# Softmax denominators inverted once per head and query, in a transformer block on one Trainium2 core

## The chip, the cores and the metric

The kernel runs on one core of one Trainium2 chip. The metric is the device time of one execution in microseconds (us). Besides the timed runs there is one execution taken by the hardware profiler; all rows below are of that one. The engines are named as in the profile: PE (TensorE, matrix products; PEld are its weight loads), DVE (VectorE), ACT (ScalarE), POOL (GpSimd) and SP (the queue that issues most transfers).

## The reference, cut to what matters

One block of a transformer with adaptive layer norm, on x of 4 x 2048 x 256 in float32:

```python
h = layernorm(x) * (1 + ca) + sa
q, k, v = heads(h @ w_qkv)                       # 8 heads of 32
scores = q @ k.T / sqrt(32) + head_scale * q_proj * k_proj, causal
x = x + ga * (softmax(scores) @ v) @ w_out
h = layernorm(x) * (1 + cb) + sb
p = softmax(h @ router_w.T); gate = its 4 largest of 16, the rest 0
x = x + gb * (shared_experts(h) + sum over e of gate[e] * expert_e(h))   # gelu inside
```

The softmax divides, for each head and query, a sum over keys of exp(score - max) * v by the sum of exp(score - max), the denominator. This division is what the change rewrites.

## The kernel before, in words

The 8192 tokens are cut into 16 blocks of 512 queries; block i is query block qb = i % 4 of its batch row, so it looks at (qb + 1) * 4 tiles of 128 keys. Heads come in two groups g of four (NQ = 2), each head in 32 partitions.

Everything is emitted in an order written out by the program: each engine executes its instructions strictly in that order (`Pinned`, L41). The order comes from a planner with costs in us: `T_US, P_US, M_US, M_VE, S_US = 0.6, 1.8, 1.05, 2.7, 3.2`. Block i is emitted as a part i of two stretches, called fill i and sum i below.

- **Fill i** (`fill_in`, L517): "pieces" of PE work (projections of a later block, the output product of block i-1, the shared expert of block i-2, routed expert tiles) between "tops", the searches for row maxima of block i+1. One search is four score products on PE, a mask where needed, and two `TENSOR_REDUCE` of 128x1024 on DVE. The planner counts 1.05 us of PE and 2.7 or 3.4 us of DVE for it, and puts the first search when its clock passes `begin`. `begin` is 5.0, or, where a lead of projections comes first, the length of that lead plus 1. `whole = begin + sum(ve of all searches)`; routed expert tiles are taken into the fill by `take_tiles(max(whole - own, backlog - 90.0))`, where `own` is the planned time of the other pieces. Searches that find no cover are left to the sum.
- **Sum i** (`sum_steps`, L665): ks = 8 * (qb + 1) steps. A step makes scores again (tile `st`), subtracts the maxima by a small product, takes exp on ACT (tiles `p`), and adds p @ v into one PSUM tile (`av`) and p @ ones into another (`dv`). As `ones` is 128 x 32, every denominator stands 32 times: in the 32 partitions of its head, the query along the columns.

At the last key tile DVE copies the denominators to SBUF (`rd<-dv`, L746) and ACT copies the numerators (`oT<-av`). The two accumulators alternate in two PSUM tiles (`accp`), so the next head group's products, or the next fill's, wait for these copies. Then come four `divide` steps per head group (L750): a `RECIPROCAL` of 128x128 in place and a product of 128x128. Those of the first head group are put into the second half of the sum, those of the second (`ends`) between the first pieces of the next fill. `rd` has one buffer.

`put` (L1501) places DVE work beside the steps of a sum: every step has 2.2 us of `room` (1.4 beside a search), and a piece takes its cost from it; a `divide` counts 1.2. Where 2.2 us are left in two neighbouring steps, the kernel "joins": DVE adds two p tiles (two `TENSOR_TENSOR p<-p,p` of 128x1024), and one set of `dv` products serves both key tiles.

**Routing.** The 14 first blocks form groups of 2, 3, 3, 3 and 3. Once a group's last block has chosen its experts, `place_steps` gives every row its place, and POOL scatters the rows into a DRAM buffer (`xg<-rows,at`, one indirect DMA for 128 rows, each paced behind ACT's latest instruction). The calls stand in the list `scatters`, and `tick()` issues one of them at a time: once or twice a step of a sum, every 3.2 planned us in a fill. When the list is empty, which is looked at after a fill and after a sum, `tiles_of(group)` makes the group's expert tiles ready: from then on a fill may take them. A set of four tiles needs rows (`xr<-xg`, SP, which waits for all scatters of the group), weights of four experts (`wt<-experts`, SP, 4 x 256 KB), turns (`px`), up (`pu`), gelu, down (`py`) and a store (`yg<-y`). Rows and weights are fetched two sets ahead. The last fill, 15, takes whatever is left. Behind sum 15 stands the dense tail for the last two blocks, with the last group's tiles.

Of the kernel before, what the change touches and what calls it, by code (L numbers as in the profile page):

```python
# [12 lines left out]
F32 = mybir.dt.float32  # L13
# [6 lines left out]
P = 128  # L20
# [14 lines left out]
def run(placed):  # L35

    for _, step in sorted(placed, key=lambda p: p[0]):
        step()
# [54 lines left out]
def adaln_block_kernel(  # L93
# [405 lines left out]
    def tick(add=True):  # L499
        for due in sums_due:  # L500
            due[0] -= 1
        if add and sums_due and sums_due[0][0] <= 0:
            sums_due[0][1].pop(0)()
            if not sums_due[0][1]:
                sums_due.pop(0)
        if scatters:
            scatters.pop(0)()
            return
        if not gathers and ready and len(sums_due) < 2:
            gathers.extend(ready[0][0])  # L510
        if gathers:
            gathers.pop(0)()
            if not gathers:
                sums_due.append([3, ready.pop(0)[1]])
# [150 lines left out]
    def sum_steps(i, g, oT):  # L665


        qb = i % NB
        nkb = (qb + 1) * TT
        qT, mT = qTs[i], mTs[i, g]  # L670
        sums = []
        pts, held = {}, {}
        joining = set()

        def keys(kb):
            return (i - qb + kb // TT) % SLOTS, kb % TT

        def left(kb):
            return max(0, kb - qb * TT) * P

        def probabilities(kb):
            lo = left(kb)
            slot, n = keys(kb)
            halves = [pair(f"st{i}_{g}_{kb}_{a}") for a in range(2)]
            heads = [both[:, u, :] for both in halves for u in range(2)]
            for h in range(4):
                r = G * h
                nc.tensor.matmul(
                    heads[h][:, lo:],
                    lhsT=kT[r : r + G, slot, g, n * P : (n + 1) * P],  # L690
                    rhs=qT[r : r + G, g, lo:],
                    start=True,
                    stop=False,
                    tile_position=(r, 0),
                )
            for h in range(4):
                r = G * h
                nc.tensor.matmul(
                    heads[h][:, lo:],
                    lhsT=unit3[r : r + 3, :],  # L700
                    rhs=mT[r : r + 3, lo:],
                    start=False,
                    stop=(kb < qb * TT),
                    tile_position=(r, 0),
                )
            if kb >= qb * TT:
                for h in range(4):
                    nc.tensor.matmul(
                        heads[h][:, lo : lo + P],
                        lhsT=ident_b,  # L710
                        rhs=kmask,
                        start=False,
                        stop=True,
                    )
            pts[kb] = []
            for a, both in enumerate(halves):
                name = f"p{i}_{g}_{kb}_{a}"
                if kb in joining:
                    pt = probs.tile([P, 2, QB], F32, bufs=2, tag="joins", name=name)
                else:  # L720
                    pt = probs.tile([P, 2, QB], F32, tag="pt", name=name)
                nc.scalar.activation(pt[:, :, lo:], both[:, :, lo:], AF.Exp)
                pts[kb].append(pt)

        def weigh(kb, s):
            if len(sums) == s:
                sums.append(accp.tile([P, QB], F32, tag="acc", name=f"{'ad'[s]}v{i}_{g}"))
            lo = left(kb)
            slot, n = keys(kb)
            if s and kb + 1 in joining:  # L730
                return
            of = pts[kb - 1] if s and kb in joining else pts[kb]
            for h in range(4):
                r = G * h
                c0 = g * P + r
                nc.tensor.matmul(
                    sums[s][r : r + G, lo:],
                    lhsT=ones if s else vA[:, slot, n, c0 : c0 + G],
                    rhs=of[h // 2][:, h % 2, lo:],
                    start=(of is pts[0]),  # L740
                    stop=(kb == nkb - 1),
                    tile_position=(0, r),
                )
            if kb == nkb - 1 and s:
                held["rd"] = once.tile([P, QB], F32, tag="rd", name=f"rd{i}_{g}")
                nc.vector.tensor_copy(held["rd"], sums[1])  # L746
            elif kb == nkb - 1:
                nc.scalar.copy(oT[:, g, :], sums[0])

        def divide(t):  # L750
            own = slice(t * P, (t + 1) * P)
            rd = held["rd"]
            nc.vector.reciprocal(rd[:, own], rd[:, own])
            nc.vector.tensor_tensor(oT[:, g, own], oT[:, g, own], rd[:, own], ALU.mult)

        def join(kb):
            for one, other in zip(pts[kb - 1], pts[kb]):
                nc.vector.tensor_tensor(one, one, other, ALU.add)

        steps = [  # L760
            [
                lambda kb=kb: probabilities(kb),
                lambda kb=kb: weigh(kb, 0),
                lambda kb=kb: weigh(kb, 1),
            ]
            for kb in range(nkb)
        ]
        return steps, [lambda t=t: divide(t) for t in range(TT)], joining, join

    def out_steps(i, oT):  # L770

# [647 lines left out]
    for i in range(NBLK):  # L1419
# [4 lines left out]
        if i:  # L1424
            soon, later = projected_in(i)
            outs = out_steps(i - 1, oT)
            turns, ups, downs = [], [], []
            if i > 1:
                turns = turn_steps(i - 2)
                ups, downs = dense_steps(i - 2)  # L1430
            begin = 5.0
            lead, mid = [], []
            if soon:
                new = project_steps(soon[0])
                lead = new[:2] + turns[:2] + new[2:6]
                begin = sum(us for us, _ in lead) + 1.0
                mid = ups + turns[2:] + new[6:]
            elif later:
                new = project_steps(later[0])
                mid = new[:2] + turns[:2] + ups + new[2:3] + turns[2:] + new[3:]  # L1440
            else:
                mid = turns[:2] + ups + turns[2:]
            if soon and later:
                mid += project_steps(later[0])
            finals = [s for two in zip(downs, outs) for s in two] if downs else outs
            at = max(6, len(mid) - len(finals))
            tail = merged(mid[at:], finals) if mid[at:] else finals
            mid = mid[:at] + tail

            for n, s in enumerate(ends):  # L1450
                (lead or mid).insert(2 * n + 1, (0.001, s))
            tops = [] if last else maxima(i + 1)
            state["pairs"] = not last
            own = sum(us for us, _ in lead + mid)
            whole = begin + sum(ve for ve, _, _ in tops)
            backlog = sum(us for us, _ in tiles_to_come)
            now = take_tiles(1e9 if last else max(whole - own, backlog - 90.0))
            filler = own + sum(us for us, _ in now)
            m, busy = 0, begin
            while m < len(tops) and (  # L1460
                busy + tops[m][0] <= filler + 2.0 or len(tops) - m > int(0.9 * ks)
            ):
                busy += tops[m][0]
                m += 1
            rest = tops[m:]
            left = fill_in(lead + (merged(mid, now) if now and mid else mid), tops[:m], begin)
# [34 lines left out]
        def put(steps, lo, hi):  # L1501
            at, shift = int(lo), (hi - lo) / max(1, len(steps))
            for n, (us, wait, step) in enumerate(steps):
                at = min(max(at + wait, int(lo + n * shift)), ks - 1)
                while room[at] < us and at < ks - 1:
                    at += 1
                room[at] -= us
                part.append((at + 0.6, step))
            return at
# [2 lines left out]
            us = [0.6] * TT + [0.2] + [0.4] * TT + [0.0] * TT  # L1512
            return [(u, 1 if n == TT + 1 else 0, s) for n, (u, s) in enumerate(zip(us, steps))]

        put([(1.2, 0, s) for s in divided], ks // NQ + 1, ks // NQ + 1)
        if qb == 0:
            for j in fresh[:1]:
                put(norm(first_norm_steps(j)), 1, 1)
# [42 lines left out]
        if 0 < i < 4:  # L1561
            now = tables[:3] if i == 1 else tables[:8]
            tables = tables[len(now) :]
            part += [(when(length * (n + 0.7) / len(now)), s) for n, s in enumerate(now)]
        run(part)
        state["summing"] = False
        if filled is not None and not scatters:
            tiles_of(filled)
# [86 lines left out]
```

## Time and profile before

| what | us |
|---|---|
| timed runs, median of 3 | 2529.13 (2527.44 to 2539.77) |
| the profiled execution's own time | 2556.92 |
| its span, first to last instruction | 2555.2 |
| PE busy in it | 2384.5 (93%) |
| DVE busy in it | 1503.9 (59%) |
| mean granted PE clock | 0.955 |

The stretches by their first score and last score product of a block in the trace (us from the span's start): fill 9 1184.7 to 1298.3, sum 9 to 1344.8, fill 10 to 1398.1, sum 10 to 1506.7, fill 11 to 1555.7, sum 11 to 1657.2; fill 13 1757.4 to 1862.1, sum 13 to 1913.1, fill 14 to 1957.9, sum 14 to 2072.8, fill 15 to 2183.5, sum 15 to 2279.9, then the tail to 2555.2.

Nearly all instructions are recorded at one line, L52, because the helper `Pinned` issues them; they are told apart by their tiles. A group of the profile names line, engine, operation, out<-in, shapes and count, then the busy time and the mean ns of one, then the engine's idle time before them and what ended it. A row of the windows view gives a stretch, its length, the busy time and instruction count of PE, PEld, DVE, ACT and POOL, the granted PE clock, and the share and rate of the DMA engines. A matmul in float32 is recorded as two passes, and four of 32 rows or 32 columns run side by side.

### The profile page before, as it was taken

Reading aid. Unit: us, or ns where it says so; the run is one execution under the profiler, and the core shown is the slowest. Engines: PE = TensorE matmul, PEld = TensorE weight load, DVE = VectorE, ACT = ScalarE, POOL = GpSimd, SP = SyncE. Lnnn points to the kernel's source line nnn. Section 1 sums busy time; section 2 is a strip of 40 time slices with the busy share of each in tenths; the row PEclk is TensorE's granted clock in tenths of the full one; section 3 lists DMA queues with packets and bytes.
Section 4 is the critical chain, followed back from the end, with each engine's and each line's share of the span. In section 5 each row is a group of like instructions: output and inputs, shape, how many; then the busy total and the mean of one; then the engine's idle time right before and its main releaser. Section 6 shows DMA issues by size and latency. Waiting matters only on the chain. (4 is left out here: it accounts for less than half of the span.)

```text
span 2555.2 us, 42456 instructions
## 1 busy us (share of the span) xinstructions
PE 2384.5 (93%) x16713; PEld 1181.2 (46%) x16713; DVE 1503.9 (59%) x2895; ACT 980.1 (38%) x1391; POOL 714.9 (28%) x740
## 2 busy tenths in 40 slices
PE   7999999999999999999999999998998998998987
PEld 4443433345544333365645344364633257435754
DVE  5576665546667775547575657658557840552235
ACT  2324244543333344534353345533342344552320
POOL 3201010511124035201013333502353320454334
PEclk9989999999999899999999999998997999998999
DMA  3200403233532112233622145233623259337943
GB/s 118 87 1 9 149 9 124 104 133 111 179 100 65 34 50 95 71 116 121 211 96 75 51 142 160 86 125 113 224 88 103 63 181 305 127 118 265 332 147 115
DMA packets 219704, 306.90 MB, mean 120 GB/s; under 512 B 18544, under 2 KB 158832, under 8 KB 219504
## 3 DMA queue, kind: packets, MB, share of 16 engines
q1 hardware_dynamic: 192720, 228.89, 27.1%
q0 software_dynamic: 25536, 73.43, 9.0%
q8 instruction: 132, 2.16, 0.4%
q10 hardware_dynamic: 1248, 1.86, 0.2%
q14 instruction: 68, 0.56, 0.1%
HBM read 193.49 MB, written 114.82 MB: 121 GB/s over the span
## 5 line engine op out<-in xcount | busy, mean ns | idle before, releaser
L52 DVE TENSOR_REDUCE parts<-ps 128x2 f32<-128x1024 f32 (+3 forms) x640 | 662.4, 1063 | 314.6 <-PE ps L52 305.4
L52 ACT ACTIVATE p<-st 128x1024 f32<-128x1024 f32 (+3 forms) x640 | 538.9, 894 | 624.4 <-PE st L52 530.1
L52 PE MATMUL st<-qT,kv 32*128 32x512 f32 (+3 forms) x2560 | 423.6, 588 | 18.3 <-ACT p L52 11.7
L52 PE MATMUL ps<-kv,qT 32*128 32x512 f32 (+3 forms) x2560 | 398.8, 610 | 25.9 <-DVE parts L52 16.2
L52 POOL DMA_INDIRECT got<-yg,at x224 | 222.6, 994 | 358.3 <-ACT p L52 100.1
L52 PE MATMUL av<-p,kv 128*32 128x512 f32 (+3 forms) x2560 | 309.0, 549 | 4.4 <-DVE rd L52 2.0
L72 POOL DMA_INDIRECT xg<-rows,at x219 | 219.0, 1000 | 290.4 <-ACT p L52 121.3
L52 PEld LDWEIGHTS st<-qT,kv 32*128 32x128 f32 x2560 | 152.1, 186 | 282.6 <-issue 167.6
L52 PE MATMUL dv<-p,ones 128*32 128x512 f32 (+3 forms) x2312 | 267.7, 535 | 1.6 <-DVE p L52 1.6
L52 PEld LDWEIGHTS ps<-kv,qT 32*128 32x128 f32 x2560 | 133.9, 192 | 233.0 <-issue 99.1
L52 DVE TENSOR_TENSOR ps<-ps,cmask 128x256 f32<-128x256 f32 x256 | 109.3, 427 | 224.3 <-PE ps L52 187.7
L52 POOL TENSOR_TENSOR x<-x,tmps 128x512 f32<-128x512 f32 x28 | 35.4, 1263 | 520.2 <-DVE tmps L52 520.1
L52 PE MATMUL st<-mT,unit 3*128 3x512 bf16 (+3 forms) x1280 | 175.0, 348 | 0.0
L52 PE MATMUL pu<-xt,wt 128*128 128x128 f32 x1216 | 157.3, 280 | 16.3 <-DMA wt<-experts 14.5
L52 PE MATMUL py<-wt,tact 128*128 128x256 f32 x608 | 164.0, 403 | 8.8 <-DVE rd L52 1.9
L52 PEld LDWEIGHTS pu<-xt,wt 128*128 128x128 f32 x1216 | 148.8, 192 | 38.4 <-issue 13.9
L52 ACT COPY y<-py 128x512 f32<-128x512 f32 x152 | 89.0, 586 | 146.9 <-PE py L52 145.8
L52 PEld LDWEIGHTS py<-wt,tact 128*128 128x128 f32 x608 | 111.0, 196 | 51.2 <-issue 8.5
L52 PEld LDWEIGHTS dv<-p,ones 128*32 128x32 f32 x2312 | 63.5, 110 | 148.3 <-issue 137.1
L52 DVE RECIPROCAL rd<-rd 128x128 f32<-128x128 f32 x128 | 121.0, 945 | 0.9
L52 PEld LDWEIGHTS av<-p,kv 128*32 128x32 f32 x2560 | 53.8, 108 | 140.8 <-issue 117.0
L52 POOL TENSOR_TENSOR x<-x,tmp 128x512 f32<-128x512 f32 x32 | 40.5, 1267 | 278.1 <-DVE tmp L52 238.8
(289 smaller groups left out, 2588.9 us busy)
## 6 DMA issues: line engine op xcount, KB each, us to landing
wt<-experts SPq DMA_DIRECT2D x304, 256.0 KB
xr<-xg SPq DMA_DIRECT2D x76, 512.0 KB
yg<-y SPq DMA_DIRECT2D x76, 512.0 KB
xg<-zeros SPq DMA_DIRECT2D x16, 1024.0 KB
xin<-in_x SPq DMA_DIRECT2D x16, 512.0 KB
x<-in_x SPq DMA_DIRECT2D x16, 512.0 KB
h2d<-xnb POOLq DMA_DIRECT2D x14, 512.0 KB
pre<-x POOLq DMA_DIRECT2D x14, 512.0 KB
```

Source lines behind the costliest of these rows:

```text
L52: made = call(*args, **kwargs)
L72: made = call()
```

## The change

- The copy of the denominators becomes a DVE transpose: each square of 32 partitions by 32 columns is turned, so that a query stands in a partition and the 32 equal copies along the columns.
- `invert` takes the reciprocal of the first column of each of the 16 squares (128x16) into a small tile `each`; `back` turns squares made of that column repeated 32 times, and so puts the reciprocals where they are needed.
- `divide` remains a product, now two of 128x256. The four steps go where the four `divide` steps went; `put` counts 0.2, 0.7, 0.5, 0.5 instead of 1.2 each.
- `begin` of a fill without a lead is 2.5 instead of 5.0.
- After a sum, when one or two scatters are left, they are issued at once, so that `tiles_of` follows before the next fill instead of after it.

```diff
@@ -742,16 +742,28 @@
             if kb == nkb - 1 and s:
                 held["rd"] = once.tile([P, QB], F32, tag="rd", name=f"rd{i}_{g}")
-                nc.vector.tensor_copy(held["rd"], sums[1])
+                nc.vector.transpose(held["rd"], sums[1])
             elif kb == nkb - 1:
                 nc.scalar.copy(oT[:, g, :], sums[0])
 
-        def divide(t):
-            own = slice(t * P, (t + 1) * P)
-            rd = held["rd"]
-            nc.vector.reciprocal(rd[:, own], rd[:, own])
-            nc.vector.tensor_tensor(oT[:, g, own], oT[:, g, own], rd[:, own], ALU.mult)
+        def invert():
+            each = small.tile([P, QB // G], F32, bufs=1, tag="each", name=f"each{i}_{g}")
+            squares = held["rd"].rearrange("p (b j) -> p b j", j=G)
+            nc.vector.reciprocal(each, squares[:, :, 0])
+            held["each"] = each
+
+        def back():
+            squares = held["rd"].rearrange("p (b j) -> p b j", j=G)
+            wide = held["each"].unsqueeze(2).broadcast_to([P, QB // G, G])
+            nc.vector.transpose(squares, wide)
+
+        def divide(half):
+            own = slice(half * QB // 2, (half + 1) * QB // 2)
+            nc.vector.tensor_tensor(oT[:, g, own], oT[:, g, own], held["rd"][:, own], ALU.mult)
...
-        return steps, [lambda t=t: divide(t) for t in range(TT)], joining, join
+        return steps, [invert, back, lambda: divide(0), lambda: divide(1)], joining, join
@@ -1428,7 +1440,7 @@
-            begin = 5.0
+            begin = 2.5
@@ -1512,7 +1524,7 @@
-        put([(1.2, 0, s) for s in divided], ks // NQ + 1, ks // NQ + 1)
+        put([(us, 0, s) for us, s in zip((0.2, 0.7, 0.5, 0.5), divided)], ks // NQ + 1, ks // NQ + 1)
@@ -1563,6 +1575,8 @@
         run(part)
+        while filled is not None and 0 < len(scatters) <= 2:
+            tick()
         state["summing"] = False
         if filled is not None and not scatters:
             tiles_of(filled)
```

## The prediction

> **What bounds the kernel now.** First the page's busy times.
>
> ```profile
> PE 2384.5 (93%) x16713; PEld 1181.2 (46%) x16713; DVE 1503.9 (59%) x2895; ACT 980.1 (38%) x1391; POOL 714.9 (28%) x740
> ```
>
> PE is the bound and DVE is not, so DVE time saved is not time saved. Next the groups by form, for prices.
>
> ```profile
> L52 PE MATMUL dv<-p,ones 128*32 128x512 f32 x1544 | 206.6, 610 | 1.6 <-DVE p L52 1.6
> L52 DVE RECIPROCAL rd<-rd 128x128 f32<-128x128 f32 x128 | 121.0, 945 | 0.9
> L52 DVE TENSOR_TENSOR oT<-oT,rd 128x128 f32<-128x128 f32 x128 | 42.2, 330 | 6.8 <-DVE rd L52 0.5 <-ACT oT L52 0.2
> L52 DVE TENSOR_TENSOR sum<-sum,gbs 128x256 f32<-128x256 f32 x56 | 24.4, 435 | 0.8
> L52 DVE COPY rd<-dv 128x512 f32<-128x512 f32 x32 | 22.0, 687 | 89.0 <-PE dv L52 62.9 <-PE ptb L52 17.1 <-PE pta L52 8.9
> L52 DVE RECIPROCAL rsm<-rsm 128x4 f32<-128x4 f32 x16 | 2.9, 178 | 0.6
> ```
>
> Then the windows view, by stretch: fill 9, sum 11, fill 14, sum 14, fill 15, sum 15 (length; busy PE, PEld, DVE, ACT, POOL; clock).
>
> ```profile
> 1184.70:1298.30 113.60, 106.05 (x678) 69.71 (x670) 70.76 (x98) 38.97 (x68) 13.39 (x15) 0.97 0.62 203
> ...
> 1555.70:1657.20 101.50, 96.90 (x831) 30.50 (x830) 77.94 (x172) 59.43 (x68) 54.62 (x52) 0.97 0.35 106
> ...
> 1913.10:1957.90 44.80, 39.33 (x200) 21.09 (x192) 31.83 (x38) 5.70 (x10) 18.11 (x18) 0.79 0.43 144
> 1957.90:2072.80 114.90, 110.04 (x855) 33.69 (x854) 88.02 (x167) 43.45 (x51) 40.05 (x43) 0.96 0.20 61
> 2072.80:2183.50 110.70, 94.00 (x628) 81.30 (x620) 16.51 (x34) 49.03 (x89) 9.87 (x9) 0.98 0.85 283
> 2183.50:2279.90 96.40, 93.09 (x845) 30.36 (x845) 49.08 (x106) 58.32 (x67) 52.96 (x52) 1.00 0.29 91
> ```
>
> The average hides this: fill 14 has too little PE work (clock 0.79), sum 14 is then loaded with searches (DVE 88 of 115), and fill 15 has tiles and hardly any DVE work (16.5 of 111) while DMA is at 0.85. The waits view gives the reason for fill 15's idle PE:
>
> ```profile
> PE pu L52 <- DMA wt<-experts: 14.5, 17, 2.0
> ```
>
> Of these, 13.6 us lie in fill 15. Last the timeline after a group's last scatter, in the tail and where fill 14 begins:
>
> ```profile
> 2316.58 0.96 POOL L72 DMA_INDIRECT xg<-rows,at  x1 [0.30 <-issue]
> ...
> 2319.22 0.92 SPq L52 DMA_DIRECT2D xr<-xg  x2
> ...
> 2323.55 1.94 PE L52 MATMUL px<-ident,xr 128*128 128x128 f32 x8 [8.11 <-DMA xr<-xg]
> ```
> ```profile
> 1918.75 1.82 PE L52 MATMUL ptb<-ident,xnb 128*128 128x128 f32 x8 [2.39 <-ACT oT L52]
> ...
> 1921.47 0.96 POOL L72 DMA_INDIRECT xg<-rows,at  x1 [0.85 <-ACT h2T L52]
> ...
> 1923.88 0.92 SPq L52 DMA_DIRECT2D xr<-xg  x2
> ```
>
> From scatter to rows takes 2.6 + 4.3 us.
>
> **The division.** Per head group it cost 0.687 + 4 x (0.945 + 0.330) = 5.79 us of DVE. The reciprocal of 16 columns, from its two rows: (945 - 178) / 124 = 6.2 ns a column, 178 + 12 x 6.2 = 0.25 us. Two products at 0.435. No row shows a DVE transpose: below, the COPY of the same shape and source, 0.69; above, the reciprocal's rate, 0.178 + 508 x 0.0062 = 3.3 us. I take 0.69, since both only move data. New: 0.69 + 0.25 + 0.69 + 0.87 = 2.50, a saving of 3.29, 105 us of DVE over 32 head groups. (The Trainium skill, VectorE: DVE Perf Modes, "The three transpose paths", gives 311 ns for 128x128 in bf16; with 384 more columns at the COPY's 1.34 ns that is an estimate of 0.83 us, and 9 us more of DVE; no run here shows it.) PE hides nearly all of it. What shows are PE waits ended by `rd`, 8.4 us over the trace, four of them near 1.9 us (fills 5, 9, sum 5, fill 15): the copy stands on DVE behind older divides and the PSUM tile comes free late. 6.5 of them lie outside part 14/15; I take 5.
>
> **Joins.** `put` charges 1.9 instead of 4.8. Going through its rooms as written I get 39 joins for 31 (the 62 rows p<-p,p are 31 joins): 6 more in sum 14, 1 in sum 15, one net elsewhere. A join saves one `dv` set: 206.6 / 1544 x 4 = 0.53 us of PE.
>
> **begin.** Fills 1, 2 and 6 have more search than PE work, so the planner's clock, within 7% of the trace there (45.5, 52.0, 52.0 planned; 42.5, 49.0, 51.9 in the trace), falls by 1.8, 2.6 and 2.6. In fills 9 to 13 a few tiles and three searches change places (planned +1.3 for the fills; three searches fewer in sums, at (105.7 - 75) / 21 = 1.5 us each by sum 2 and the 75 us worked out below for such a sum without searches, -4.5). Together -10; I take 8. The next limit there is PE's own chain of transposes and copies, 2 to 4 us a fill.
>
> **The flush, the largest term.** Counting ticks, the group of blocks 8 to 10 has 51 calls and one is left behind sum 13; the trace agrees, the scatter at 1921.47 stands behind fill 14's first `ptb`. So `tiles_of` came after fill 14, which ran without tiles. With the flush fill 14 takes 84.3 planned us of 86.4, all 32 searches fit there, sum 14 keeps none of its 21, fill 15 keeps 2.1 us. Elsewhere no sum ends with one or two. Priced by stretch (before: 44.8 + 114.9 + 110.7 + 96.4 = 366.8):
>
> - Fill 14: fill 9 is the model, 113.6 us for 26.2 own, 54.0 of tiles, 24 searches. Tiles +30.3 x 0.934 (fill 15's PE busy 94.0 for 100.6 planned), own -11.4, 8 searches at 1.14 us (the timeline's set of score products): 139.6, less its `rd` wait, 137.7.
> - Its start: PE executes `px` of the new tiles first, and all of fill 14's PE work, the first search too, stands behind it. Sum 13's products ended at 1916.4. The flushed scatter stands behind `oT` and two scatters on POOL, so it starts near 1920.9; SP issues the rows at 1923.3; they land at 1927.6. Stall 11 us, against 2.4 before. Behind `xr` on SP wait the eight weight loads, needed 2 to 5 us later, as in the tail, where they added nothing. After the tail's 8.1 us wait:
>
> ```profile
> 2315.00:2324.00 9.00, 0.89 (x5) 0.52 (x4) 2.27 (x4) 0.00 (x0) 7.54 (x11) 0.68 0.52 170
> 2324.00:2330.00 6.00, 6.00 (x24) 4.03 (x24) 0.00 (x0) 1.17 (x2) 2.23 (x3) 0.63 1.02 381
> ```
>
>   so 6 us at 0.63 lose 2.2 more. The Trainium skill (TensorE: Matmul & The Clock Gate, Part 1) says that PE runs at half clock after an idle window of about 3.4 us until one busy window has passed; it speaks against this edit, the rows agree, and by it the loss is 1.7 in place of 2.2. Fill 14: 137.7 + 11 + 2.2 = 151.
> - Sum 14, without searches: between sum 9 (46.5, one join) and the mean of sums 15 and 11 without their joins (100.7, 106.8) half-way is 75.3, less 6 joins, 72. Its gathers have 72 us instead of 115, the pace of sum 15.
> - Fill 15 like fills 3 and 7 (18.6, 18.7 for 17.6 planned), now 16.3 planned without searches to fill gaps: 18.5.
> - Sum 15: 95.9.
>
> Sum 337.4, so -29. Ends: -40 if fill 14 loses no clock and the idle of fill 9 doesn't repeat; -12 if only idle PE and joins count (rival one).
>
> **Sum.** 29 + 8 + 5 + 0.5 (one join) + 1 (the tail's divides ahead of the router's DVE chain) = 43 us. 2556.9 - 43 = 2514 for a profiled execution; the median stands at 2529.13 / 2556.92 = 0.989 of it: 2487.
>
> **Rivals.**
> 1. *PE has no slack, only waits go.* If PE's busy time is true work everywhere, moving searches from sum to fill saves nothing: -13.6 (weights) -1.7 -4.2 (8 joins) -6.5 (`rd`) +11 (start) = -15, so 2514. For it: 93% busy. Against: searches cost 1.14 us in a fill and 1.5 to 1.9 in a sum ((114.9 - 75) / 21), and fill 14's busy PE runs at 0.79.
> 2. *The transposes are slow.* Place: DVE between the last `dv` and the free accumulator, 32 times. At the reciprocal's rate a head group costs 3.3 + 0.25 + 3.3 + 0.87 = 7.7, 1.9 more than before, and the accumulator comes free 2.6 us later, which is what the `rd` waits are made of: 32 x 2.6 = 83 against 29 + 8 saved, +46 us, 2575. It decides from (37 + 12.6) / 32 = 1.55 us above the COPY, 2.2 us a transpose.
> 3. *The flush never fires*, because lighter divides shift the placing of scatters so that none or three are left. I count one both ways. Then 8 + 5 + 1 + 1 = 15: 2514.
>
> **How the numbers follow.** Forecast 0.80, rival one 0.10, two 0.06, three 0.04. Differences under 0.5% (12.6 us, about what a measurement of this kernel can tell from no change) count as same, so the limit is 2516.5. Faster: nearly all of the forecast, half of rivals one and three, 0.85; same 0.09; slower 0.06. The range: below, -40 for the flush, -10, -8.4, and up to 12 of DVE relief in searching sums that I counted at nothing, -70 scaled, 2460; above, rivals one and three at 2514, so 2515.
>
> **What would show it.** Right: `rd` rows near 0.7 us twice 32, one RECIPROCAL of 128x16 near 0.25; 78 rows p<-p,p; `px` in fill 14 at once, with one wait near 11 us on `xr`, no row of `wt` waits near 14; fill 15 under 22 us, sum 14 near 72 with DVE far below 88. Wrong: transposes over 2 us, fill 14 above 165 us, or tiles still in fill 15.

## The result, and the profile after

| | us |
|---|---|
| before, median (with the changed kernel's runs beside it) | 2531.24 (2527.44 to 2539.77) |
| changed, median | 2495.93 (2495.41 to 2496.37) |
| ratio | 0.9852, 95% interval 0.9832 to 0.9873 |
| forecast | 2487, range 2460 to 2515 |

The change made the kernel 1.5% faster: 37 us of 2531 by the ratio, 35 us between the two medians.

The kernel before takes 2552 us on the chip of experiments 1 to 4, 2533 on that of experiments 5 to 8 and 2553 on that of experiments 9 to 12, so every ratio is taken against the kernel before on the same chip, and the 61 us between the spans of the two profiles (2555.2 and 2493.7) are more than the change.

The page of the changed kernel, and its groups by form that answer to those of the division:

```profile
PE 2334.9 (94%) x16649; PEld 1159.1 (46%) x16649; DVE 1430.4 (57%) x2783; ACT 980.6 (39%) x1391; POOL 730.0 (29%) x740
```
```profile
L52 DVE TENSOR_TENSOR p<-p,p 128x1024 f32<-128x1024 f32 x78 | 99.3, 1313 | 27.2 <-PE av L52 26.8 <-ACT p L52 0.3
...
L52 DVE TENSOR_TENSOR oT<-oT,rd 128x256 f32<-128x256 f32 x64 | 27.7, 458 | 2.9
...
L52 DVE STREAM_TRANSPOSE rd<-dv 128x512 f32<-128x512 f32 x32 | 22.8, 712 | 78.4 <-PE dv L52 78.3
...
L52 DVE STREAM_TRANSPOSE rd<-each 128x512 f32<-128x512 f32 x32 | 22.7, 709 | 0.9
...
L52 DVE RECIPROCAL each<-rd 128x16 f32<-128x16 f32 x32 | 8.0, 251 | 0.9
```

DVE's transpose (`STREAM_TRANSPOSE`, all squares of 32 x 32 in 128x512) takes 0.71 us, from PSUM or from a small tile read 32 times over, against 0.69 for the copy it replaces. The reciprocal of 128x16 takes 0.251 us (worked out: 0.25). A head group's division is 0.712 + 0.251 + 0.709 + 2 x 0.458 = 2.59 us for 5.79. The 78 rows are 39 joins.

The windows view by stretch: sum 12, fill 14, sum 14, fill 15, sum 15.

```profile
1698.50:1728.10 29.60, 23.41 (x226) 8.96 (x225) 16.41 (x61) 12.80 (x19) 3.35 (x3) 0.83 0.30 95
...
1890.90:2038.20 147.30, 128.29 (x866) 88.00 (x864) 80.62 (x94) 49.38 (x88) 22.95 (x24) 0.94 0.77 253
2038.20:2106.40 68.20, 67.59 (x640) 22.42 (x640) 52.30 (x117) 43.74 (x52) 41.55 (x39) 1.00 0.31 92
2106.40:2130.60 24.20, 22.10 (x110) 16.42 (x108) 8.19 (x16) 6.18 (x11) 10.27 (x11) 0.79 0.26 80
2130.60:2224.70 94.10, 92.51 (x836) 29.54 (x835) 55.94 (x115) 58.23 (x67) 57.17 (x53) 0.98 0.28 91
```

Fill 14 now holds the tiles and all searches, sum 14 runs with a full PE and a clock of 1.00, fill 15 is short. Sum 12 is a surprise: 29.6 us where the kernel before took 19.7:

```profile
1737.70:1757.40 19.70, 19.45 (x226) 8.08 (x226) 18.33 (x62) 10.94 (x17) 2.34 (x2) 1.00 0.06 20
```

The timeline shows what each of the two stalls waits for. Fill 14:

```profile
1892.54 0.58 ACT L52 COPY oT<-av 128x512 f32<-128x512 f32 x1 [0.64 <-PE av L52]
...
1894.29 0.99 POOL L72 DMA_INDIRECT xg<-rows,at  x1 [0.30 <-issue]
...
1901.91 0.96 POOL L72 DMA_INDIRECT xg<-rows,at  x1 [0.30 <-issue]
1904.31 0.91 SPq L52 DMA_DIRECT2D xr<-xg  x2
...
1908.49 1.94 PE L52 MATMUL px<-ident,xr 128*128 128x128 f32 x8 [15.80 <-DMA xr<-xg]
```

ACT is done at 1893.1, but POOL still works off scatters: seven start 1.27 us apart, from 1894.3 to 1901.9, and PE stands still for 15.8 us. Sum 12:

```profile
1700.20 2.96 SPq L52 DMA_DIRECT2D wt<-experts  x4
...
1703.70 0.51 SPq L52 DMA_DIRECT2D xin<-in_x  x1
```
```profile
1711.76 0.43 DVE L52 BATCH_NORM_STATS2 sta<-xin 128x6 f32<-128x256 f32 x1 [8.18 <-DMA xin<-in_x]
...
1715.40 0.26 ACT L52 ACTIVATE rpr<-rpr 128x64 f32<-128x64 f32 x1 [6.24 <-DVE rpr L52]
...
1716.62 1.01 PE L52 MATMUL st<-qT,kv 32*128 32x384 f32 x2 [4.06 <-ACT p L52]
```

On SP the load of a later block's input stands behind four weight loads, and those wait for a set of tiles that ends only as the sum begins. The input lands some 8 us after its load was issued. DVE waits 8.2 us for it, the router's exp on ACT waits for DVE, the softmax's exp behind it, and PE for that.

### The profile page after: what moved, and what is told of

Same layout as the page of the kernel before. It is cut to its first block, busy times and chain, and to the rows that moved or that the text cites. A ratio compares the mean times of both kernels' runs of the same rounds, so it can differ in the third digit from the quotient of the medians.

```text
span 2493.7 us, 42195 instructions
## 1 busy us (share of the span) xinstructions
PE 2334.9 (94%) x16649; PEld 1159.1 (46%) x16649; DVE 1430.4 (57%) x2783; ACT 980.6 (39%) x1391; POOL 730.0 (29%) x740
## 4 chain that ended last, share of the span: by engine, by line
PE 81%; DVE 7%; ACT 3%; issue 3%; POOL 3%; DMA 2%; SPq 0%; POOLq 0%; ACTq 0%; DVEq 0%
PE st L52 17%; PE ps L52 13%; PE av L52 10%; PE dv L52 8%; PE pu L52 8%; PE py L52 6%; DVE parts L52 3%; PE po L52 3%; PE ppq L52 2%; PE pv L52 2%; PE px L52 2%; PE ppk L52 2%; PE pd_s L52 2%; PE pd L52 2%; POOL xg L72 1%
## 5 line engine op out<-in xcount | busy, mean ns | idle before, releaser
L52 PE MATMUL st<-qT,kv 32*128 32x512 f32 (+3 forms) x2560 | 410.0, 585 | 16.0 <-ACT p L52 12.4
L52 PE MATMUL ps<-kv,qT 32*128 32x512 f32 (+3 forms) x2560 | 385.3, 604 | 18.9 <-DVE parts L52 13.3
L52 PEld LDWEIGHTS st<-qT,kv 32*128 32x128 f32 x2560 | 146.3, 186 | 273.7 <-issue 155.9
L52 PE MATMUL dv<-p,ones 128*32 128x512 f32 (+3 forms) x2248 | 258.4, 533 | 2.8 <-DVE p L52 2.8
L52 PEld LDWEIGHTS ps<-kv,qT 32*128 32x128 f32 x2560 | 127.4, 190 | 205.7 <-issue 98.4
L52 PE MATMUL st<-mT,unit 3*128 3x512 bf16 (+3 forms) x1280 | 167.4, 348 | 0.0
L52 ACT COPY xt<-px 128x512 f32<-128x512 f32 x152 | 86.2, 586 | 127.2 <-PE px L52 127.1
L52 PE MATMUL px<-ident,xr 128*128 128x128 f32 x608 | 92.9, 284 | 34.0 <-DMA xr<-xg 26.3
L52 POOL TENSOR_TENSOR xnb<-xnb,gm 128x256 f32<-128x256 f32 x128 | 105.7, 832 | 49.4 <-issue 20.6
```

The lines of the kernel that those rows point to most:

```text
L52: made = call(*args, **kwargs)
```

## The experiments

Edits are against the changed kernel unless the kernel before is named.

**1. The kernel before, again.**

> The kernel before, unchanged, for a second profile of it. The first profiled execution took 2557 us, the timed runs 2531. If that difference is a chance of one execution, this one lies near 2531 and its stretches differ from the first profile by 26 us in all, fill 14 to sum 15 near 367 us again. If the profile itself slows this kernel, it lies near 2557 again.

2552.06 us for the profiled run, where the other runs on this chip have a median of 2552.35, so it is not the profiler that makes it long. Its stretches fill 14 to sum 15 are 41.1 + 114.4 + 110.2 + 99.8 = 365.5 us (366.8 in the first profile): this part is stable.

**2. The flush alone**, in the kernel before:

```diff
         run(part)
+        while filled is not None and 0 < len(scatters) <= 2:
+            tick()
```

> The kernel before with the flush of one or two scatters alone; old division, old charges, begin 5.0. My theory (the flush is the largest term; fill 14 to sum 15 shrink by some 30 us because searches get cheap cover): 22 to 30 us faster than before, ratio 0.988 to 0.991, 36 joins. Rival one (only idle PE time and joins count): the stall on xr eats the waits on wt, 0 to 8 us faster. Rival two (the gain is DVE relief by the division): no more than 10 us faster.

2526.38 us, ratio 0.989 (0.9876 to 0.9905): 28 us of 2552 by the ratio, 26 between the medians. Windows view, fill 14 to sum 15:

```profile
1918.10:2065.10 147.00, 133.09 (x882) 90.46 (x880) 86.08 (x106) 51.03 (x90) 17.35 (x17) 0.95 0.74 242
2065.10:2141.20 76.10, 72.53 (x647) 23.77 (x646) 53.87 (x118) 43.35 (x51) 44.20 (x42) 0.99 0.36 108
2141.20:2159.80 18.60, 17.07 (x104) 12.42 (x100) 8.45 (x14) 5.50 (x10) 7.05 (x7) 0.91 0.13 39
2159.80:2260.40 100.60, 94.86 (x845) 30.57 (x845) 54.19 (x117) 58.23 (x67) 57.76 (x55) 0.98 0.28 89
```

342.3 us against 365.5: 23 us less (the profiled runs as a whole differ by 20). Rivals one (at most 8) and two (at most 10) of that expectation fall. Most of the change's gain is the flush. And it is not idle time that goes: over these four stretches PE's busy time falls from 339.1 to 317.6 us, though the joins take away only 40 of its some 2500 instructions. The same 256 score products of the searches (`ps`) take 36.7 us of PE in place of 46.8. So busy time was not a fixed amount of work; why the same products take less of it was not taken apart.

**3. The new division alone**, with the old charges, `begin` and no flush, so that all other work keeps its order:

```diff
-            begin = 2.5
+            begin = 5.0
...
-        put([(us, 0, s) for us, s in zip((0.2, 0.7, 0.5, 0.5), divided)], ...)
+        put([(1.2, 0, s) for s in divided], ...)
...
-        while filled is not None and 0 < len(scatters) <= 2:
-            tick()
```

> The new division alone: transposes, one reciprocal of 128x16, two products; the steps are charged 1.2 each as before, begin 5.0, no flush, so the order of all other work is the old one and there are 31 joins. It takes some 100 us of DVE away. My theory (PE bounds, only the waits on rd go): 3 to 8 us faster, ratio 0.997 to 0.999. Rival two (DVE relief is the gain): 15 to 30 us faster.

2547.64 us, ratio 0.998 (0.9964 to 0.9996): 5 us, with 1 to 9 in the interval. DVE's busy time fell from 1502.4 (experiment 1) to 1403.3:

```profile
PE 2384.6 (93%) x16713; PEld 1180.1 (46%) x16713; DVE 1403.3 (55%) x2767; ACT 980.8 (38%) x1391; POOL 715.2 (28%) x740
```

99 us off DVE buy 5 us of time, and PE is as busy as before (2386.3 in experiment 1). But the way was not the one I named: idle PE time ended by `rd`, added over the trace, is 10.1 us here and 7.7 in experiment 1. The two profiled runs differ by 1 us only (spans of 2551.4 and 2550.4), so they cannot tell where the 5 us lie.

**4. The changed kernel without the flush.**

```diff
-        while filled is not None and 0 < len(scatters) <= 2:
-            tick()
```

> The changed kernel without the flush: new division, new charges, begin 2.5. 33 joins, the tiles of blocks 8 to 10 run in fill 15 again. My theory: 8 to 14 us faster than before, and some 25 us slower than the changed kernel. Rival one: as fast as the changed kernel within 10 us. Rival two: 25 us faster than before or more.

2543.91 us, ratio 0.9976 (0.9959 to 0.9993): 6 us faster than before, a little less than I expected. With 0.989 for the flush alone the parts multiply to 0.987, the whole is 0.985. Sum 12 is 28.4 us here: its stall belongs neither to the flush nor to one chip.

**5. The changed kernel again**, on the chip of the next three, which are compared with it.

> The changed kernel again, as the yardstick of this call: ratio to before 0.983 to 0.987.

2493.36 us, ratio 0.9843 (0.9825 to 0.9861).

**6. `begin` back to 5.0.**

```diff
-            begin = 2.5
+            begin = 5.0
```

> The changed kernel with begin 5.0 again. In the trace of the changed kernel sum 12 is 10 us longer than before and fills 12 and 13 4 us each: DVE waits 8 us for the next block's input, whose load stands on SP behind weight loads, which wait for a set of tiles that now ends at the very end of fill 12. If begin's shuffling of tiles makes that stall, it is gone here: sum 12 near 20 us, and what begin saves elsewhere (8 us by my prediction, fills 1, 2, 6) is lost: 3 us faster to 3 us slower than the changed kernel. If the stall has another cause (the lighter division), sum 12 stays near 29 and this kernel is some 8 us slower than the changed one.

2488.43 us, ratio 0.9838 (0.9819 to 0.9856): 5 us below the changed kernel, within the two intervals. Fill 9 is 110.8 us again instead of 103.3, but sum 12 is whole:

```profile
1709.70:1729.40 19.70, 19.44 (x225) 8.03 (x224) 17.21 (x62) 10.94 (x17) 3.31 (x3) 1.00 0.08 27
```

So `begin` gives in one place what its moved tiles take in another: fill 9 and sum 10 are 7.5 and 4.7 us longer here than in experiment 5, and fill 12, sum 12 and fill 13 are 4.0, 7.9 and 8.9 us shorter. PE's wait for `xr` in fill 14 is 9.2 us here, as in experiment 2, and 15.3 in experiment 5.

**7. Own pieces first after a flush.** Fill 14 runs its 14 us of other pieces, then the tiles:

```diff
-            left = fill_in(lead + (merged(mid, now) if now and mid else mid), tops[:m], begin)
+            if state.pop("flushed", False):
+                woven = mid + now
+            else:
+                woven = merged(mid, now) if now and mid else mid
+            left = fill_in(lead + woven, tops[:m], begin)
...
+        state["flushed"] = filled is not None and 0 < len(scatters) <= 2
         while filled is not None and 0 < len(scatters) <= 2:
```

> The changed kernel, but after a flush the next fill runs its own pieces (14.2 planned us) first, with searches between them, and the tiles behind them. If the 15.8 us wait of px on xr in fill 14 is latency that other PE work can cover: that wait is under 3 us, fill 14 is 12 to 16 us shorter (131 to 136), 10 to 15 us faster than the changed kernel. If fill 14 is bound otherwise (weights, DVE), the time comes back as waits later in the fill: fill 14 above 142, less than 5 us faster.

2480.97 us, ratio 0.9788 (0.9773 to 0.9803), 12 us faster than the changed kernel. Fill 14:

```profile
1887.70:2022.20 134.50, 128.12 (x869) 86.65 (x866) 80.48 (x94) 49.41 (x88) 22.30 (x23) 1.00 0.84 277
```

PE is as busy as in the first trace of the changed kernel (128.1 for 128.3), the stretch is 12.8 us shorter, the clock 1.00 for 0.94, and no wait for `xr` is left there: the wait was latency, and other work covers it.

**8. Inputs loaded early.**

```diff
+            coming = [j for js in projected_in(i + 1) for j in js if 2 < j < NBLK]
+            (lead or mid).insert(2, (0.0, lambda: [load_in(j) for j in coming]))
             for n, s in enumerate(ends):
...
-        for j in fresh:
-            load_in(j)
         if i == 0:
+            for j in fresh:
+                load_in(j)
```

> The changed kernel with the loads of the next blocks' inputs issued early in the fill instead of behind it, so that they stand ahead of the last weight loads on SP. If the stall of sum 12 is this queue: sum 12 near 20 us, 7 to 11 us faster than the changed kernel. If something else holds DVE there: sum 12 near 29, no difference.

2481.64 us, ratio 0.9795 (0.9782 to 0.9808), 12 us faster. Sum 12:

```profile
1694.00:1713.90 19.90, 19.35 (x225) 8.02 (x224) 16.46 (x61) 12.80 (x19) 3.34 (x3) 1.00 0.37 114
```

The queue on SP is shown as the cause. Sum 11 is shorter too, 91.3 us for 96.0 in experiment 5. It repeats (92.0 in experiments 11 and 12, which have the edit; 98.0 and 99.2 in 9 and 10, which lack it), but experiment 7 had 94.2 without it, and its cause was not looked into.

**9. Every transpose twice.**

```diff
                 nc.vector.transpose(held["rd"], sums[1])
+                nc.vector.transpose(held["rd"], sums[1])
...
             nc.vector.transpose(squares, wide)
+            nc.vector.transpose(squares, wide)
```

> The changed kernel with each of the 64 transposes executed twice: 64 x 0.71 = 45 us more of DVE, and each dv accumulator comes free 0.7 us later. My theory (PE hides the division's DVE time but for the waits on rd): 0 to 8 us slower than the changed kernel, ratio to before 0.984 to 0.988. Rival two (DVE time in the division is time): 30 to 45 us slower, ratio 0.996 to 1.002.

2534.30 us, ratio 0.9927 (0.9901 to 0.9953). The changed kernel itself did not run on this chip, so the cost of 45 us more of DVE is only bounded. The kernel is 27 us slower than experiment 11, which has two gains that it lacks. Of these, 21 us lie in the stretches that those two edits shorten: sum 11 (98.0 for 92.0), sum 12 (30.8 for 19.9) and fill 14 (145.8 for 141.4). That leaves some 5 us by the medians, or 9 by the profiled runs, as an estimate of the cost. The 30 to 45 us of rival two do not fit; my 0 to 8 does, as far as this tells.

**10. The old charges.**

```diff
-        put([(us, 0, s) for us, s in zip((0.2, 0.7, 0.5, 0.5), divided)], ...)
+        put([(1.2, 0, s) for s in divided], ...)
```

> The changed kernel with the four steps charged 1.2 each again, so 37 joins for 39 and slightly other places for the DVE steps. By my price of 0.53 us a join 1 us slower than the changed kernel, within 4 us of it in all; if the freed room is worth more than the joins, 5 us slower or more.

2532.02 us, ratio 0.9932 (0.9906 to 0.9959). The changed kernel on the same chip is missing here too. By stretches, sum 7 takes 110.3 us, against 103.4 in experiment 11 and 103.5 in experiment 4, which have the new charges, and 109.6 in experiment 3 with the old ones; sum 3 takes 108.3 against 106.6, 106.5 and 108.3. The joins are the same there (6 and 4), so in these two sums the freed room is worth more than joins: the DVE steps stand elsewhere, and with the new charges a wait of PE of 2.0 us for a search's maximum is gone from each. Other stretches go the other way (fill 10 56.9 us for 62.9 in experiment 11, sum 5 53.6 for 56.9). Outside sum 11, sum 12 and fill 14, which the edits of experiment 11 shorten, this kernel is only 6 us behind experiment 11 by the medians and 2 by the profiled runs, so what the charges are worth as a whole stays open.

**11. Experiments 7 and 8 together.**

> Own pieces first after a flush, and early loads of the next inputs, together, on the changed kernel. The two stalls lie in different parts, so the gains should add: 20 to 25 us faster than the changed kernel, ratio to before 0.974 to 0.976. If one only moves the other's wait, less than 15 us.

2507.68 us, ratio 0.9825 (0.9800 to 0.9849). Sum 12 is 19.9 us as in experiment 8, fill 14 141.5 and not 134.5. The gain is less than expected (a ratio of 0.974 to 0.976). The changed kernel on this chip is unknown, so whether the two gains add up stays open; both stalls are gone from the trace.

**12. And the tail.** Five pieces of the dense experts ahead of the last group's tiles:

```diff
-    fill_in(free(norms) + merged(rest[:30], amid[:9]) + ..., pace=2.4, add=True)
+    fill_in(free(norms) + amid[:5] + merged(rest[:30], amid[5:9]) + ..., pace=2.4, add=True)
```

> The same, and in the tail five pieces of the dense experts (7.7 planned us) go ahead of the last group's first tiles, where PE waits 10.5 us for xr. If that wait is latency like fill 14's: it falls to 2 to 4 us, 5 to 9 us faster than both edits alone, ratio 0.971 to 0.973. If the tail is bound by its transfers and gathers behind it: no difference, the span's end waits for got instead.

2504.12 us, ratio 0.9820 (0.9794 to 0.9846). The tail shrinks from 274.0 to 267.5 us and PE's wait for `xr` there is gone, but the whole is only 3.6 us faster, within the intervals of the two, and without this edit the tail took anything from 268.7 to 275.3 us in the other profiles. So a gain is not shown.

## Why the prediction was right, point by point

- **What bounds it.** Held. 99 us of DVE are worth 5 us (experiment 3).
- **The division's prices.** Held: 2.59 us for 2.50 worked out. The Trainium skill (VectorE: DVE Perf Modes, "The three transpose paths") gives 311 ns for 128x128 in bf16, from which the estimate of 0.83 us for a transpose came; the trace has 0.71, so the COPY's row was the better price.
- **The flush, 29 us.** Held in sum: 28 us alone (experiment 2), and in the changed kernel fill 14 to sum 15 take 147.3 + 68.2 + 24.2 + 94.1 = 333.8 us for 337.4 forecast. Part of that is luck, since mis-sized terms cancel. The stall at the start was 15.8 us and not 11, because I let two scatters stand on POOL where there were six ahead of the last one; with `begin` at 5.0 it is 9.2 (experiments 2 and 6), so the longer queue came with the shift of `begin`. Fill 15 was 24.2 us and not 18.5, above the 22 that I had named as a sign. Fill 14 without its stall (131.5 for 140) and sum 14 (68.2 for 72) were shorter. Between two traces of one chip (experiments 1 and 2) the four stretches fall by 23 us, not 29.
- **The clock after the stall.** As forecast, 2.6 us lost for 2.2. Behind the wait, fill 14 has these rows:

```profile
1908.50:1914.50 6.00, 6.00 (x32) 5.46 (x32) 0.00 (x0) 3.04 (x4) 0.99 (x1) 0.56 1.05 377
1914.50:1920.50 6.00, 5.71 (x37) 3.53 (x38) 3.47 (x4) 2.75 (x5) 1.92 (x2) 1.00 0.75 242
```

  The Trainium skill (TensorE: Matmul & The Clock Gate, Part 1) says half clock until a busy window has passed. The trace agrees: 0.56 in these 6 us, 1.00 in the next 6. By the 0.56, half clock lasted 5.3 us here, and so cost more than the 1.7 us that the prediction worked out from one window.
- **`rd` waits, 5 us.** The size held by luck, the reason fell: experiment 3 is 5 us faster, but its waits on `rd` are not shorter (10.1 us for 7.7). What gave the 5 us was not found.
- **`begin`, 8 us.** This step failed: experiment 6 finds no gain. I added up the planner's clock and priced a few tiles that change places at their PE time, and did not follow what queues behind them. One set of tiles then ended at the end of fill 12, the loads queued behind it on SP cost sum 12 8 to 10 us, and fills 12 and 13 grew. Of the fills I counted on for 7 us, fills 2 and 6 gain some 1.5 us each (47.8 for 49.3, 48.1 for 49.5 in experiments 5 and 6), fill 1 nothing (39.1, 39.0). The searches that leave the sums do pay (sum 10, 4.7 us, in experiment 6). Experiment 8, which keeps `begin` at 2.5 and takes the stall away, is 7 us below experiment 6 by the medians; early loads with `begin` at 5.0 were not run, so how much of that is `begin` stays open.
- **Joins.** 39 as counted, in the sums that I named. DVE relief in searching sums, which I put at nothing with up to 12 us in the range, shows in sums 3 and 7 with the new charges. Charges and `begin` together are worth 4 us (experiment 4 against 3), within the intervals.
- **Rivals.** One (only waits go) fell with experiment 2: PE's busy time itself fell, and the products of the searches took less of it. Two (slow transposes) fell by the rows. Three (no flush) fell: the tiles are in fill 14.

The forecast was 9 us low (2487 for 2496). The failed 8 us of `begin` are about that much, but other terms were off both ways, so that the rest came out so near is partly luck.

## What to carry to other kernels

Where one engine is the bound, look for stretches in which it has too little to do and others in which its work lacks cover; moving a block of work from one to the other was worth 28 us here, more than five times what 99 us off a second engine were. When work moves, follow everything that queues behind it: the flush put PE's first instruction behind a chain of seven scatters and a load, and a shift of one set of tiles put an input load behind weight loads that waited. Each gave 12 us back after a reorder of a few lines: either cure alone gives a kernel of 2481 or 2482 us, beside 2493 for the changed one on the same chip.

## What the runs showed of the hardware that was not expected

- A scatter of 128 rows occupies POOL for 0.96 us and the next starts 1.27 us after the start of the one before, so a few in a row are a latency of their own: seven took 8.6 us.
- A DVE transpose of 128x512 in float32, in squares of 32 x 32, costs within 4% of the copy of the same shape (0.712 for 0.687 us), also with a source of stride 0 (0.709 us).
- The kernel before has medians of 2552, 2533 and 2553 us on three chips. On the first and the third the traces show ACT waits ahead of the softmax's exp that nothing in the program ends, 25 to 30 us in all; on the second at most 3.3 us. Experiment 1 has this row:

```profile
ACT p L52 <- issue: 28.6, 12, 2.9
```

  What these waits are was not found, nor whether they make the difference; each chip ran at another time, so chip and time are not told apart.
